# Turning two of four heads' softmax weights by VectorE blocks and DMA in the third attention of a four-layer conditioned sequence model

## The chip, the cores and the metric

The kernel runs on one core of one Trainium2 chip, as one program. The metric is the device time of one execution in microseconds (us). A program on one core is timed several times and the median is used; beside it there is one profiled execution, from which the page and every answer of the trace come.

A core has five engines with a queue of instructions each: TensorE (PE; its weight loads, PEld, overlap the matmuls), VectorE (DVE), ScalarE (ACT), GpSimd (POOL) and SyncE (SP), which here issues every DMA.

## The reference, cut to what matters

The input is `x` of 8 items with 256 tokens of 512 features. Four layers run in turn: a grouped attention with gated feed-forward (8 query heads, one key head), an attention with 16 heads and a feed-forward, the attention below, and a layer of small experts. The third layer is what the change bears on:

```python
h = h * (1.0 + scale[:, None, :]) + shift[:, None, :]      # h: layer norm of x
q = (h @ Wq.T).reshape(B, T, N_HEADS, HEAD_DIM).transpose(0, 2, 1, 3)      # 16 heads of 32
c_kv = h @ Wkd.T
k = (c_kv @ Wku.T).reshape(B, T, N_KV_HEADS, HEAD_DIM).transpose(0, 2, 1, 3)   # 4 heads
v = (c_kv @ Wvu.T).reshape(B, T, N_KV_HEADS, HEAD_DIM).transpose(0, 2, 1, 3)
...
scores = jnp.einsum('bhtd,bhsd->bhts', q, k_exp) / jnp.sqrt(jnp.asarray(HEAD_DIM, x.dtype))
scores = jnp.where(mask[None, None], jnp.asarray(-jnp.inf, x.dtype), scores)
attn = jax.nn.softmax(scores, axis=-1)
y = jnp.einsum('bhts,bhsd->bhtd', attn, v_exp)
out = y.transpose(0, 2, 1, 3).reshape(B, T, C) @ Wo.T
return x + out
```

The mask hides every key block of 128 that lies after the query's block. So the first 128 queries see 128 keys, the second 128 see 256.

## The kernel before, in words

**Layout.** Tokens are kept in 16 tiles of 128 tokens x 512 features in SBUF (`x`), two tiles (TB = 2) to an item. All arithmetic is fp32. The three attentions share one routine, `attend` (line 652 on). "Item" below means one of the 8 batch items, and "group" four heads of it that are worked on together. The third attention ("attention2", called in `layer2`, line 1673) has 4 groups an item, so 32 groups.

**One group.** `scored` (line 680; matmuls L692) gives the scores of four heads, queries on partitions, in four PSUM banks. `softmax` (line 698) has VectorE add the mask and find each row's maximum in one masked reduce per head and query block (L730), and ScalarE take the exponential with its row sum (L734). In this attention a head has 128 + 256 = 384 columns. The weights must then stand with the keys on partitions, as the second matmul sums over keys. There are two ways for that:

- *By TensorE* (`turned`, line 764). Each 128x128 tile is transposed by a matmul with the identity into a PSUM bank (L769), three tiles a head here, and the bank is copied back to SBUF by `copy` (line 474): VectorE for an even index (L478), ScalarE for an odd one (L481). The index starts at 0 with four such heads and at 1 with two.
- *By blocks* (in `softmax`, L739 to L743). Two heads' exponentials are written interleaved in 32-column blocks into one tile; VectorE transposes all its 32x32 blocks in one instruction (L739); four DMAs write it to a DRAM buffer, exchanging blocks (`put`, line 542, issued at L546); one DMA reads it back (L743). For this the heads' keys are read in another order in `scored`, and the bias or mask must be in the same order (`biased[1]`).

`weighted` (line 776, matmuls L794) multiplies values and turned weights: for each key tile the heads 0 to 3 in turn. `divided` (L811) divides by the row sums, which come by a small transposition (L745, L749) and two DMAs (L752, L757). `in_blocks` (line 538) says how many of the four heads go by blocks: two in the first and second attention, except in the last item, and none in the third.

**The order.** The loop of `attend` is pipelined by one group: scores of group i, first half of the turning of group i-1, softmax of group i, second half of the turning of i-1, weighting of i-1. Between these steps `some(quantum)` takes pieces of other work from a queue of Python generators: the output product of the item before (`added`, line 1288), the projections of the next item (`project2`, line 1633), and extra work. A generator yields the time it estimates for a piece, or None, after which `some` (line 207) ends; the forced `rest()` at each item's first group empties the queue and doesn't end on None.

**The tokens of an item ahead.** At an item's first group `prepare` (line 517) is begun for the item after next: `norms` (line 439) finds means and variances and normalises two token tiles into the buffer `hT`, yielding before each of them; then VectorE transposes hT's blocks (L532) and `put` writes it to DRAM. One step of it is taken per group. `fetch` (line 550), called once a group, reads it back with eight DMAs (L564), and `modulate` applies scale and shift at the item's last group (L488, L489).

**What is issued.** The text's order is not the issued order: a planner (the framework's scheduler) orders each engine's instructions by the text's order as priority and by when it expects them to be ready. `keep_in_program_order` (line 587, and line 803 for the weighting of heads that go by blocks) holds an instruction behind what stands before it on its engine in the text.

**The rotary tables** of the first layer are made by `angles` (line 1153) with VectorE and ScalarE: for the first item's tiles before the loop, and for the last 12 tiles in `conditions(0)` (line 1298), a generator queued behind the projection of item 1.

Of the kernel before, what the change touches and what calls it, by code (L numbers as in the profile page):

```python
# [34 lines left out]
P = 128  # L35
B, S, D = 8, 256, 512
NT = B * S // P
# [55 lines left out]
def in_blocks(m):  # L93

    return np.ascontiguousarray(m.reshape(-1, TB, 4, 32).transpose(0, 2, 1, 3).reshape(len(m), -1))


def constants():

    f32 = np.float32  # L100
    freqs = (f32(1.0) / f32(10000.0) ** (np.arange(0, 32, 2, dtype=f32) / f32(32))).astype(f32)
    ang = np.arange(S, dtype=f32)[:, None] * freqs[None, :]
    cos = np.cos(ang.astype(np.float64)).astype(f32)
    sin = np.sin(ang.astype(np.float64)).astype(f32)
    rope = np.stack([np.concatenate([cos, cos], 1), np.concatenate([-sin, sin], 1)], 1)
    rope = rope.reshape(TB, P, 2, 32).transpose(1, 0, 2, 3)
    i, k = np.arange(S)[:, None], np.arange(S)[None, :]
    hidden = ((np.abs(k - i) > 64) & (k % 64 != 0)) | (k // P > i // P)
    mask = np.where(hidden, f32(MASKED), f32(0.0))
    mask = np.concatenate([mask[:P, :P], mask[P:, :]], 1)  # L110
    return {
        "inv_freq": np.array([INV_FREQ], f32),
        "rope2": np.ascontiguousarray(rope),
        "mask2": np.ascontiguousarray(mask),
    }


# [61 lines left out]
class Program:  # L179
    def __init__(self, ctx, tc, d, out):  # L180
        self.ctx, self.tc, self.nc, self.d, self.out = ctx, tc, tc.nc, d, out
        self.n = 0
        self.queue, self.credit = [], 0.0
        self.ready, self.calls = {}, 0

    def pool(self, name, psum=False):
        return self.ctx.enter_context(
# [251 lines left out]
    def norms(self, xs, eps, rms=False, outs=None):  # L439


        nc = self.nc
        n = len(xs)
        mv = self.t([P, n, 2], f"mv{n}", 2)
        r = self.t([P, n], f"r{n}", 2)
        for i, x in enumerate(xs):
            st = self.t([P, 6], "st", 3)
            nc.vector.bn_stats(st, x)  # L448
            nc.vector.bn_aggr(mv[:, i, :], st)  # L449
        mean, var = mv[:, :, 0], mv[:, :, 1]  # L450
        if rms:
            nc.vector.tensor_tensor(r, mean, mean, ALU.mult)
            nc.vector.tensor_tensor(r, r, var, ALU.add)
            nc.gpsimd.tensor_scalar(r, r, eps, None, ALU.add)
        else:
            nc.gpsimd.tensor_scalar(r, var, eps, None, ALU.add)  # L456
        nc.gpsimd.tensor_tensor(r, r, self.neg_half[:, 0:n], ALU.pow)
        rows = []
        for i, x in enumerate(xs):
            yield  # L460
            if outs is None:
                y = self.bank("n")
            else:
                y, x = outs[i], x.rearrange("p (k c i) -> p c k i", k=KC, c=4)
            if rms:
                nc.vector.tensor_scalar(y, x, r[:, i : i + 1], None, ALU.mult)
            else:
                nc.vector.tensor_scalar(
                    y, x, mv[:, i, 0:1], r[:, i : i + 1], ALU.subtract, ALU.mult
                )  # L470
            rows.append(y)
        return rows
# [64 lines left out]

    def in_blocks(self, name, b):

        return 2 if name != "attention2" and b < B - 1 else 0  # L540

    def put(self, kept, tile):

# [6 lines left out]
    def fetch(self, calls):  # L550

        for (name, b), entry in self.ready.items():
            hT, _, kept, _, _ = entry
            if kept is None:
                continue
            entry[2:4] = None, self.calls + calls
            if self.stage(name)[5]:
                self.nc.sync.dma_start(hT, kept)
                continue
            parts = kept.rearrange("p (a k t j) -> p k t a j", a=4, k=KC, t=TB)  # L560
            to = hT.rearrange("p (k t a j) -> p k t a j", k=KC, t=TB, a=4)
            for k in range(KC):
                for t in range(TB):
                    self.nc.sync.dma_start(to[:, k, t], parts[:, k, t])  # L564

# [584 lines left out]

    def angles(self, cos, sin, tiles):

        nc = self.nc
        n = tiles.stop - tiles.start
        shape = [P, n, 32]
        cos, sin = cos[:, tiles], [s[:, tiles] for s in sin]
        pos = self.t([P, NT], "posf", 1)[:, 0:n]
        nc.vector.tensor_copy(pos, self.pos[:, tiles])  # L1160

        ang, high, rest = sin[1], sin[0], cos
        low = self.t([P, NT, 32], "n")[:, 0:n]
        nc.vector.tensor_tensor(
            ang,
            pos.unsqueeze(2).to_broadcast(shape),
            self.inv_freq.unsqueeze(1).to_broadcast(shape),
            ALU.mult,
        )

        def rounded(k, of, period):
            nc.vector.tensor_scalar(k, of, 1.0 / period, ROUND, ALU.mult, ALU.add)
            nc.vector.tensor_scalar(k, k, ROUND, None, ALU.subtract)

        def less(out, k, c):
            nc.vector.scalar_tensor_tensor(out, k, -c, ang, ALU.mult, ALU.add)

        rounded(high, ang, PERIOD)
        for c in HIGH[:3]:
            less(ang, high, c)  # L1180
        less(rest, high, sum(HIGH[3:]))
        rounded(low, rest, 2 * math.pi)
        for k, c in (
            (low, LOW[0]), (high, HIGH[3]), (low, LOW[1]), (high, HIGH[4]), (low, LOW[2]),
            (high, HIGH[5]),
        ):
            less(ang, k, c)

        rounded(low, ang, 2 * math.pi)
        less(ang, low, LOW[0])  # L1190
        less(ang, low, LOW[1] + LOW[2])
        nc.vector.tensor_scalar(ang, ang, PI_BELOW, -PI_BELOW, ALU.min, ALU.max)
        nc.scalar.activation(sin[0], ang, AF.Sin, scale=-1.0)
        nc.scalar.activation(rest, ang, AF.Abs)
        nc.scalar.activation(sin[1], ang, AF.Sin)
        nc.scalar.activation(cos, rest, AF.Sin, bias=self.half_pi, scale=-1.0)
# [98 lines left out]
    def layer0_attention(self):  # L1295
        self.ups = []

        def conditions(b):
            if b == 0:
                self.angles(self.cos, self.sin, slice(2 * TB, NT))  # L1300
                yield None
                yield from self.ada_1()
                yield from self.ada_0(1)
                self.ada_23_load()
            else:
                yield from self.ada_23()

                self.ups += [[None, None] for _ in range(8)]
                for i in (0, 1, 2, -1, 3, -2, -3, -4):
                    self.layer0_up(i if i >= 0 else -1 - i, int(i >= 0))  # L1310

        self.attend(
            "attention0", 2, 64, self.project0, lambda v, g, j, k: v[:, k, :],
            lambda b, ctxT: self.added(b, ctxT, self.w0o), (10.5, 6.8),
            extra={
                0: (conditions(0), 7.7), 2: (conditions(2), 4.6),
                5: (self.sums_of_ups(0, 2), 0.0), 6: (self.sums_of_ups(2, 4), 0.0),
                7: (self.mlp_input("mlp0"), 0.0),
            },
            then=lambda: self.mlp_begin("kept0"),  # L1320
            spare=lambda: [self.ups[i][1][:, 7, :] for i in range(4)],
            inverse=[self.w0[:, k, 640:896] for k in range(4)], after="mlp0",
        )
# [294 lines left out]
    def load_layer2(self):  # L1618
        nc, d = self.nc, self.d
        w = self.t([P, KC, 1536], "wqkv", pool=self.wqkvp)  # L1620
        self.load(w[:, :, 0:512], "wq2T")
        self.load(w[:, :, 512:640], "wkdT")
        nc.sync.dma_start(w[:, 0, 640:896], d["wkvuT"])
        self.w2 = w
        self.w2o = self.t([P, KC, D], "wo", pool=self.wop)
        self.load(self.w2o, "wo2T")
        rope = self.bank("row")[:, 0 : TB * 64].rearrange("p (t c s e) -> p t c s e", t=TB, c=2, s=2)
        nc.sync.dma_start(rope.rearrange("p t c s e -> p t c (s e)"), d["rope2"])
        self.rope2 = rope
        self.mask = self.bank("row")[:, :384]  # L1630
        nc.sync.dma_start(self.mask, d["mask2"])

    def project2(self, b, got):
        nc, w = self.nc, self.w2
# [38 lines left out]
    def layer2(self):  # L1673
# [2 lines left out]
        self.attend(  # L1676
            "attention2", 4, 32, self.project2, lambda v, g, j, k: v[:, k, j * 32 : (j + 1) * 32],
            lambda b, ctxT: self.added(b, ctxT, self.w2o), (10.4, 6.8), key_tiles=(1, 2),
            biased=(self.mask,), extra={7: (self.expert_inputs(0), 1.74)},
            spare=lambda: [spare[:, i, :] for i in range(4)],  # L1680
            inverse=[spare[:, i, :] for i in range(4, 8)],
        )
# [180 lines left out]
```

## Time and profile before

| what | value |
|---|---|
| median of 3 runs | 2106.18 us (2105.13 to 2107.4) |
| the profiled execution | 2102.78 us |
| its span, first to last instruction | 2100.7 us |
| mean granted TensorE clock | 0.989 of full speed |
| third attention, first scores to last weighting | 1673.5 to 1949 us |
| second attention, likewise | 913.3 to 1262 us |
| one item of the third, in the steady part | 34.4 us |
| one item of the second | 43.6 us |

How to read the page: its first part gives each engine's busy time and share of the span. The groups of instructions name line, engine, operation, output<-inputs by the program's tile names, shape and count, then busy time, the mean of one in ns, the idle time of the engine before them, and what ended it. In a timeline each row has a start and a length in us and may merge several instructions (x6); a note in brackets is the idle time before it and what released it. L794 and L692 appear twice per matmul of the program, so 16 records are 8 matmuls. Matmuls overlap in the array, so a record's length is not what one adds.

Some groups of the page on which this case turns:

```profile
L769 PE MATMUL C<-ident,p 128*128 128x128 f32 x816 | 122.3, 282 | 4.8 <-DVE p L478 1.9 <-ACT qT L482 1.5 <-ACT p L734 0.8
L734 ACT ACTIVATE p<-p,low 128x256 f32<-128x256 f32 (+1 forms) x512 | 240.0, 471 | 165.8 <-DVE low L730 154.5
```

L769 are the transposes by TensorE of all three attentions, 384 of the 816 in the third. In their row the idle time ahead of them is 4.8 us in all. The second row is the exponentials; ScalarE's idle time before them is mostly waiting for the reduces.

### The profile page before, as it was taken

The page shows a single profiled execution, that of the slowest core. Times are in us where ns is not written, and L with a number is a line of the kernel's source. Part 1 is how long each engine was busy: PE and PEld are TensorE (multiplying, and loading weights), DVE is VectorE, ACT ScalarE, POOL GpSimd, SP SyncE. Part 2 cuts the span into 40 slices and gives each one's busy share as a digit, 9 for nine tenths or more (in the row PEclk, how much of TensorE's full clock was granted, in tenths as well). Part 3 has the DMA queues.
Part 4 walks back from the last instruction along what each step waited for, and adds up shares of the span by engine and source line. Part 5 has one row for each costly group of instructions (what it writes and reads, how often), then busy time and mean ns, then how long its engine had stood idle before and what let it go on. Part 6 is the DMA issues. An engine that isn't in the chain of part 4 may idle for free.

```text
span 2100.7 us, 36220 instructions
## 1 busy us (share of the span) xinstructions
PE 2034.6 (97%) x12946; PEld 1486.9 (71%) x12946; DVE 1348.9 (64%) x4432; ACT 743.7 (35%) x2330; POOL 302.7 (14%) x340
## 2 busy tenths in 40 slices
PE   7799999999999999999999999999999999999999
PEld 4455569999999999854544448999999755555444
DVE  6677766666676555756676675767666777676233
ACT  4233421111111111146566652222222265556543
POOL 1111200000000000054445621000000111010220
PEclk8999999999999999999999999999999999999999
DMA  9543451212130010335455542235211321210001
GB/s 317 161 139 94 115 202 39 72 42 64 62 108 26 16 32 16 97 95 140 130 145 142 150 132 87 86 92 155 63 46 36 89 44 38 58 38 21 9 36 40
DMA packets 202659, 182.48 MB, mean 87 GB/s; under 512 B 81200, under 2 KB 169200, under 8 KB 202480
## 3 DMA queue, kind: packets, MB, share of 16 engines
q1 hardware_dynamic: 202480, 180.17, 29.3%
q8 instruction: 103, 1.69, 0.3%
q14 instruction: 76, 0.62, 0.1%
HBM read 122.16 MB, written 57.97 MB: 86 GB/s over the span
## 4 chain that ended last, share of the span: by engine, by line
PE 82%; DVE 6%; ACT 6%; DMA 3%; POOL 2%; issue 1%; SPq 0%; ACTq 0%; DVEq 0%; POOLq 0%
PE C L1002 28%; PE C L628 21%; PE A L1051 18%; ACT p L734 4%; PE A L692 4%; PE C L794 3%; PE C L769 3%; PE A L1731 1%; PE C L1750 1%; ACT p L481 1%; DVE st L448 1%; DVE p L730 1%; DMA hT<-turn 1%; PE C L315 1%; DVE n L647 1%
## 5 line engine op out<-in xcount | busy, mean ns | idle before, releaser
L1002 PE MATMUL C<-hT,wbig 128*128 128x128 f32 x3072 | 416.4, 275 | 1.0 <-DVE p L1025 1.0
L1002 PEld LDWEIGHTS C<-hT,wbig 128*128 128x128 f32 x3072 | 388.7, 192 | 10.1 <-issue 3.5
L628 PE MATMUL C<-wqkv,hT 128*128 128x512 f32 (+1 forms) x768 | 314.7, 551 | 0.4 <-ACT v L1490 0.4
L734 ACT ACTIVATE p<-p,low 128x256 f32<-128x256 f32 (+1 forms) x512 | 240.0, 471 | 165.8 <-DVE low L730 154.5
L1051 PE MATMUL A<-wbig,p 128*128 128x256 f32 x1024 | 242.2, 379 | 0.0
L628 PEld LDWEIGHTS C<-wqkv,hT 128*128 128x128 f32 x768 | 131.7, 193 | 122.7 <-issue 108.7
L1051 PEld LDWEIGHTS A<-wbig,p 128*128 128x128 f32 x1024 | 189.7, 190 | 23.1
L1032 DVE TENSOR_TENSOR p<-p,C 128x256 f32<-128x256 f32 x192 | 79.0, 419 | 164.3 <-PE C L1002 162.3
L1022 ACT COPY p<-C 128x128 f32<-128x128 f32 x192 | 50.8, 265 | 367.5 <-PE C L1002 359.0
L628 PE MATMUL C<-wo,ctxT 128*128 128x512 f32 x336 | 159.8, 609 | 2.9 <-DVE ctxT L811 2.9
L1002 PE MATMUL C<-ctxT,wbig 128*128 128x128 f32 x1152 | 160.0, 275 | 0.0
L1002 PE MATMUL C<-qk,wbig 128*128 128x128 f32 x1152 | 159.8, 275 | 0.0
L456 POOL TENSOR_SCALAR r<-mv 128x2 f32<-128x2 f32 (+1 forms) x28 | 7.0, 252 | 967.7 <-DVE mv L449 967.7
L730 DVE CUSTOM_DVE_ANT_0 p<-A,row 128x256 f32<-128x256 f32 (+1 forms) x400 | 127.8, 377 | 26.6 <-PE A L692 24.9
L1002 PEld LDWEIGHTS C<-ctxT,wbig 128*128 128x128 f32 x1152 | 144.1, 192 | 0.0
L1002 PEld LDWEIGHTS C<-qk,wbig 128*128 128x128 f32 x1152 | 144.0, 192 | 0.0
L769 PEld LDWEIGHTS C<-ident,p 128*128 128x128 f32 x816 | 92.2, 142 | 64.3 <-issue 37.8
L769 PE MATMUL C<-ident,p 128*128 128x128 f32 x816 | 122.3, 282 | 4.8 <-DVE p L478 1.9
L1374 ACT ACTIVATE p<-C 128x128 f32<-128x128 f32 x64 | 17.7, 277 | 302.4 <-DVE p L1032 302.4
L1023 DVE TENSOR_TENSOR p<-p,C 128x128 f32<-128x128 f32 x192 | 54.7, 285 | 96.6 <-ACT p L1022 95.6
L628 PEld LDWEIGHTS C<-wo,ctxT 128*128 128x128 f32 x336 | 59.5, 191 | 67.7 <-issue 55.2
L734 ACT ACTIVATION_READ_ACCUMULATOR p<-p,low 128x1 f32 x512 | 96.2, 188 | 0.0
(227 smaller groups left out, 3224.6 us busy)
## 6 DMA issues: line engine op xcount, KB each, us to landing
flip<-p SPq DMA_DIRECT2D x168, 128.0 KB
p<-flip SPq DMA_DIRECT2D x42, 512.0 KB
turn<-hT SPq DMA_DIRECT2D x120, 128.0 KB
hT<-turn SPq DMA_DIRECT2D x16, 512.0 KB
kept<-hT SPq DMA_DIRECT2D x16, 512.0 KB
hT<-kept SPq DMA_DIRECT2D x16, 512.0 KB
wbig<-spread SPq DMA_DIRECT2D x64, 128.0 KB
hT<-turn SPq DMA_DIRECT2D x112, 64.0 KB
```

The costliest lines, as they stand in the source:

```text
L315: self.nc.tensor.matmul(m[32 * i : 32 * i + 32, :], cond[:, k, :], w[c // 512][:, k, c % 512 : c % 512 + width], start=(k == 0), stop=(k = ...
L628: self.nc.tensor.matmul(out, lhsT(k), rhs(k), start=(k == 0), stop=(k == n - 1))
L692: nc.tensor.matmul(s[j][:, at[q] : at[q] + wide[q]], lhsT(q), keys, start=True, stop=True,)
L730: nc.vector.tensor_tensor_reduce(out, src, by, -1.0, BIG, ALU.add, ALU.min, low[:, q : q + 1])
L734: nc.scalar.activation(out, src, AF.Exp, bias=low[:, q : q + 1], scale=sign, accum_out=tot[:, j, q : q + 1],)
L769: nc.tensor.transpose(m[:, n * P : (n + 1) * P], p[:, at[q] + k * P : at[q] + (k + 1) * P], self.ident,)
L794: mm = nc.tensor.matmul(o[i * hd : (i + 1) * hd, c * S + q0 * P : (c + 1) * S], value(got[b][1], g, j, k), weights(j, mine), start=(k == 0 ...
L1002: nc.tensor.matmul(m[:, c : c + P], w[:, k * P : (k + 1) * P], b[:, k], start=(first and k == 0), stop=(k == steps - 1), skip_group_check= ...
L1022: nc.scalar.copy(g[:, 0, :], m[:, 0:P])
L1023: nc.vector.tensor_tensor(g[:, 0, :], g[:, 0, :], m[:, P : 2 * P], ALU.add)
L1032: nc.vector.tensor_tensor(g[:, 1:3, :], g[:, 0, :].unsqueeze(1).to_broadcast([P, 2, P]), m[:, 2 * P : 4 * P].rearrange("p (i t) -> p i t", ...
L1051: nc.tensor.matmul(acc[at][:, half * S : (half + 1) * S], left, right, start=(p == 0 and half == 0), stop=(p == 3), skip_group_check=True,)
```

## The change

1. `in_blocks` no longer excludes the third attention: in items 0 to 6 heads 0 and 1 of each group go by blocks. The mask is given in block order as well (`mask2_blocks`, a new constant of 128 x 384), and one bank now holds the rotary rows and the mask, the other the mask by blocks.
2. `norms` yields only before the second tile, so the first tile is normalised in the step that finds the statistics.
3. `fetch` reads an item's eight pieces in two calls of four, unless one of them is asked for at once or the whole is one DMA; the time from which it may be used is set at the second.
4. `angles` is a generator in four steps (`angle_steps`), and `conditions(0)` yields after each.

```diff
+        "mask2_blocks": np.concatenate([mask[:, :P], in_blocks(mask[:, P:])], 1),
...
         for i, x in enumerate(xs):
-            yield
+            if i > 0:
+                yield
...
     def in_blocks(self, name, b):
 
-        return 2 if name != "attention2" and b < B - 1 else 0
+        return 2 if b < B - 1 else 0
...
-            entry[2:4] = None, self.calls + calls
-            if self.stage(name)[5]:
+            whole = self.stage(name)[5]
+            ks = self.fetching.pop((name, b), range(KC if calls == 1 or whole else KC // 2))
+            if ks.stop == KC:
+                entry[2:4] = None, self.calls + calls
+            else:
+                self.fetching[name, b] = range(ks.stop, KC)
+            if whole:
                 self.nc.sync.dma_start(hT, kept)
                 continue
...
-            for k in range(KC):
+            for k in ks:
                 for t in range(TB):
                     self.nc.sync.dma_start(to[:, k, t], parts[:, k, t])
...
-    def angles(self, cos, sin, tiles):
+    def angles(self, *args):
+        for _ in self.angle_steps(*args):
+            pass
+
+    def angle_steps(self, cos, sin, tiles):
...
             if b == 0:
-                self.angles(self.cos, self.sin, slice(2 * TB, NT))
+
+                yield from self.angle_steps(self.cos, self.sin, slice(2 * TB, NT))
                 yield None
...
-        self.mask = self.bank("row")[:, :384]
+        self.mask = both[:, TB * 64 :]
         nc.sync.dma_start(self.mask, d["mask2"])
+        self.mask_blocks = self.bank("row")[:, :384]
+        nc.sync.dma_start(self.mask_blocks, d["mask2_blocks"])
...
-            biased=(self.mask,), extra={7: (self.expert_inputs(0), 1.74)},
+            biased=(self.mask, self.mask_blocks), extra={7: (self.expert_inputs(0), 1.74)},
```

`angle_steps` has three bare `yield`s: after the first reductions, and twice within and after the second ones.

## The prediction

> **What bounds the kernel now.** I read the page's engine row first, then the table by stretches for one batch item of the grouped attention (the third, of masked keys, 1673 to 1949 us), then the timelines of TensorE and ScalarE inside it, then the same views of the second attention, which already does what this change adds.
>
> ```profile
> span 2100.7 us, 36220 instructions
> PE 2034.6 (97%) x12946; PEld 1486.9 (71%) x12946; DVE 1348.9 (64%) x4432; ACT 743.7 (35%) x2330; POOL 302.7 (14%) x340
> ```
> TensorE is the bound over the whole span, so work taken from it looks like time. In the stretch that changes, one item (us, then busy us of PE, PEld, DVE, ACT, POOL, clock, DMA) has 1.5 us in 34.4 in which it isn't busy:
>
> ```profile
> 1779.50:1813.90 34.40, 32.85 (x232) 17.96 (x232) 24.76 (x114) 19.53 (x77) 4.30 (x6) 1.00 0.22 49
> ```
> Where these lie decides this case. TensorE's timeline of two weightings (L794) of that item:
>
> ```profile
> 1801.47 1.99 PE L628 MATMUL C<-wqkv,hT 128*128 128x512 f32 x4
> 1803.38 0.86 PE L794 MATMUL C<-p,v 128*32 128x256 f32 x16
> 1804.17 0.94 PE L692 MATMUL A<-v,qT 32*128 32x128 f32 x16
> 1805.04 0.87 PE L769 MATMUL C<-ident,p 128*128 128x128 f32 x6
> 1805.75 1.88 PE L628 MATMUL C<-wqkv,hT 128*128 128x512 f32 x4
> 1807.46 0.82 PE L769 MATMUL C<-ident,p 128*128 128x128 f32 x6
> 1808.12 0.60 PE L1652 MATMUL C<-wqkv,n 128*128 128x256 f32 x2
> 1808.75 0.63 PE L794 MATMUL C<-p,v 128*32 128x256 f32 x6
> 1809.92 0.84 PE L794 MATMUL C<-p,v 128*32 128x256 f32 x10 [0.54 <-ACT p L481]
> ```
> The first runs through in 0.86 us. The second stops after 6 of its 16 records, until ScalarE has copied the fourth head's turned weights. ScalarE's timeline shows why it is late:
>
> ```profile
> 1807.29 0.45 ACT L481 COPY p<-C 128x384 f32<-128x384 f32 x1
> ...
> 1809.32 0.19 ACT L734 ACTIVATION_READ_ACCUMULATOR p<-p,low 128x1 f32 x1
> 1809.41 0.46 ACT L481 COPY p<-C 128x384 f32<-128x384 f32 x1
> ```
> Eight exponentials and two copies run there without a gap, 4.76 us from the end of the scores (1805.1) to the end of the second copy. Measured so, from the end of the next group's scores, the four weightings of an item begin at +5.49, +5.42, +3.65 and +4.29 us, and the copy ends at +4.76, +4.56, +4.76 and +4.76: **slack 0.73 and 0.86, stall 1.1 and 0.5 us**. These repeat within 0.02 us in items 1 to 5. In item 6 two weightings stall and two have 0.05 us; in item 0 none has slack.
>
> **The change, part by part.**
>
> *Turning two of four heads elsewhere (items 0 to 6, 28 groups).* Removed: 6 of 12 transposes a group (L769). Their record says 0.28 us each, but they overlap: runs of 4 and of 8 take 0.66 and 1.09 us, so one costs 0.108 and six 0.65; 28 x 0.65 = 18.2 us of TensorE. Two VectorE copies of 0.55 go as well; ScalarE keeps both of its copies, since with two plain heads the index in `turned` gives both to it. So its 4.76 us stay, and six transposes fewer only count where a weighting has slack: the first two of an item, in items 1 to 5: 10 x 0.65 = **6.5 us**. In the other 18 groups TensorE arrives earlier and waits longer.
>
> On this the Trainium skill says ("TensorE: Matmul & The Clock Gate", Part 4: PE-mode transpose) that a 128x128 transpose takes about 275 ns inside a kernel. The records agree (273 ns median), the pitch in a run doesn't: by the page 28 x 6 x 0.275 = 46 us would leave TensorE, as an estimate.
>
> *Between two items* the scheduler fills a wait for the query copies with transposes: three, then two that wait 0.25 us for ScalarE's query copy, then the scores at 1813.89. With only three left to move there the scores can begin at 1813.53: 0.36 us, six times, **2.2 us**; 0 if other work is put in their place, 4.6 if ScalarE's first copy then also precedes its exponentials (about 0.4 more each).
>
> *What is added.* VectorE: one transpose of 128x768 a group. 128x1024 takes 1.245 us (L739), so 0.93, against 1.09 of copies: -0.16 us. VectorE is busy 24.8 of 34.4 us, so this is nothing in itself. The forms by blocks (runs of 32 or 64 elements) cost no more: in the second attention, where both occur, a weighting matmul takes 379 ns in either, a score matmul 374, an exponential 494 and 495, a masked reduce 419. SP: four writes (0.43 us each) and one read (0.34) a group, 2.1 us. TensorE's first weighting matmul now waits for that read. Behind it stand all of TensorE's later matmuls, and for them everybody.
>
> *When that read lands.* The trace has it in the second attention:
>
> ```profile
> 1175.08 1.25 DVE L739 STREAM_TRANSPOSE p<-p 128x1024 f32<-128x1024 f32 x1 [0.22 <-ACT p L734]
> ```
> ```profile
> 1176.35 1.75 SPq L546 DMA_DIRECT2D flip<-p  x4
> 1178.14 0.55 SPq L752 DMA_DIRECT2D spread<-invT  x1
> 1179.69 0.30 SPq L546 DMA_DIRECT2D turn<-hT  x1
> 1180.62 0.34 SPq L743 DMA_DIRECT2D p<-flip  x1
> ```
> Scores ended at 1172.0. Transpose at +3.1, writes from +4.3, landed at +8.5, read issued at +8.6, landed at +13.1. Over items 1 to 5 the medians of the landing are +13.4, +13.1, +12.6 and +13.1 for an item's four groups. In the grouped attention half of the reduces are 0.14 us shorter (-0.55), the transpose is 0.31 shorter, and the read is 384 KB instead of 512 (the 42 reads took 3.35 to 5.4 us, I take 0.4 off): 1.25 us earlier, so **+12.15, +11.85, +11.35, +11.85**. TensorE wants them, with the saving made, at 8.5 + 4.8 = +13.3, 8.55 + 4.8 = +13.3, 6.45 + 4.5 = +10.95, and 9.4 + 4.3 = +13.7 (distance to the next scores, plus the weighting's place; where ScalarE's copy binds, its end less 0.25). Only the third group is late, by 0.4 us: six times with item 6, 2.4 us. Item 6's first group (wanted at +11.0) adds 0.6. The very first group came at +17.1 in the second attention, here +15.9 against +14.8: 1.1. Sum **4.1 us lost**. Bounds: 1.1 if the reads land 0.4 us earlier, 12 if 1 us later.
>
> Against the whole idea the skill warns ("VectorE: DVE Perf Modes", The three transpose paths) that a plain strided DMA used as a transpose is 19 times slower than the crossbar's 1309 ns. As an estimate that is 25 us; every group would then wait over 10 us. The landing of 3.35 to 5.4 us speaks against it: these transfers move whole runs of blocks.
>
> *Tokens' blocks read by halves, norms one step earlier.* Eight reads (0.63 us on SP) become four and four; the first rows are written one group sooner. What is executed isn't the text's order: SP issues L752 before L743 above, though the text has it later. The rows are normalised when the hT buffer comes free (1779.4, just before the scores), reads issue from 1791 to 1798, and modulation uses them at 1812: 11 us of cover. Cost 0. Without cover a late read holds up VectorE and ScalarE, at most the 2.9 us for which SP once waited there. I take 0, between 1 us gained (SP freer for the new transfers) and 1 lost.
>
> *Rotary tables in steps.* The call that runs them is the forced `rest()` of item 1: the four calls of `some` in item 0 are spent on the four empty yields of the projection ahead in the queue, and `rest()` doesn't stop at empty yields. The tables' VectorE work stands at 58 to 65 us, ahead of item 1's first scores at 75, and its order stays as it is: 0.
>
> *Mask.* One more load of 192 KB. Today's mask is loaded at 1272 us and first used near 1679; the new one goes with it, and 400 us cover it: 0.
>
> **Sum.** -6.5 - 2.2 + 4.1 = -4.6 us. The profiled execution took 2102.78 us, its span 2100.7 and 2.1 around it; it becomes 2098.2. The median shown, 2106.18, is 3.4 us above that execution; the same difference gives **2101.6 us**.
>
> **Rivals.**
> *A, the whole saving:* the scheduler lets ScalarE's second copy pass the last exponentials, now that VectorE feeds them without two copies between, or reads land early. Then 18.2 us and the boundary's 2.2 go less the 1.1 at the start: down to 2087; from 2097 down counts here. For it: PE at 97%. Against: ScalarE's unbroken 4.76 us.
> *B, nothing:* ScalarE's chain and the late read eat all but 2 us either way, 2104 to 2108. For it: stall and gain are of one size.
> *C, slower:* VectorE puts the new transpose behind the reciprocal (L745), which stands at +4.45 waiting for the last exponential. The read then lands 1.9 us later than I reckon: third groups lose 2.3 us (six times, 13.8), first and second ones 0.75 and 0.45 (five times each, 6.0), item 6's first 2.5, the start 3: 25.3 - 8.7 = +16.6, or 2123. It decides from 0.6 us of delay on, where loss equals gain. For it: SP has eight further issues an item and the landings spread by 2 us. Against: in the second attention VectorE does this transpose before the reciprocal.
>
> **Chances.** Forecast (2098 to 2105) 0.50, of which 0.31 lies over 0.2% below the median and 0.19 within it; A 0.19; B 0.11; C 0.20. A measurement of this kernel can tell about 0.2%, 4.2 us. So faster 0.50, within 0.30, slower 0.20. The range, 2093 to 2113, leaves out about half of A and half of C.
>
> **What would show it.** Six-record runs of L769 become runs of three. The first two weightings of an item begin 0.65 us sooner; the other two still stop for ACT p L481. The waits table gets a row of L794 waiting for the DMA p<-flip, under 5 us in all. The new transposes stand near +2.9 of their scores, before L745. Were it over 10 us, or L739 behind L745, C is right; if the wait for L481 disappears, A.

## The result, and the profile after

| | before | after |
|---|---|---|
| median of 11 runs each | 2105.45 us | 2109.56 us |
| profiled execution, its span | 2102.78, 2100.7 us | 2109.53, 2107.4 us |
| third attention, first scores to the next layer's first matmul | 267.6 us | 272.7 us |

The ratio is 1.0020, 95% interval 1.0011 to 1.0029: **slower by 0.2%**, about 4 us, where 4.6 us less was forecast. Line numbers move with the edits; in the changed kernel L699 are the scores (L692 before), L776 TensorE's transposes (L769), L801 the weighting (L794), L548 all block writes, L571 the reads of the tokens' blocks, L750 the read of the turned weights (L743).

The page of the changed kernel, first lines:

```profile
span 2107.4 us, 36234 instructions
## 1 busy us (share of the span) xinstructions
PE 2020.4 (96%) x12778; PEld 1476.4 (70%) x12778; DVE 1352.2 (64%) x4404; ACT 744.6 (35%) x2330; POOL 303.8 (14%) x340
```

TensorE has 14.2 us less to do, and the span is longer: the time went into idle TensorE. Of the 6.7 us between the two profiled executions 5.1 lie in the third attention. Up to there TensorE's and VectorE's planned orders are those of before, and a kernel with the other parts of the change alone (below) is as fast as before. The item lengths, from one item's first scores to the next's:

| item | 0 | 1 | 2 | 3 | 4 | 5 | 6 | 7 |
|---|---|---|---|---|---|---|---|---|
| before | 37.4 | 34.1 | 34.4 | 34.4 | 34.4 | 34.4 | 28.9 | 29.4 |
| after | 41.0 | 29.7 | 35.8 | 33.4 | 37.8 | 32.7 | 27.0 | 35.3 |

Items 1, 3 and 5 gain 1.0 to 4.4 us, items 2 and 4 lose 1.4 and 3.4, item 0 loses 3.6, and items 6 and 7 together 4.0. The waits of TensorE in this attention, some of the longest (us in total, times, longest):

```profile
PE C L801 <- DMA p<-flip: 25.6, 10, 6.1
...
PE A L699 <- DVE qT L481: 3.6, 1, 3.6
PE C L801 <- ACT p L483: 1.3, 4, 0.7
```

The wait for the read of the turned weights is the new one, 25.6 us where under 5 was forecast. TensorE's timeline in item 2, which answers to the two weightings shown of before:

```profile
1768.25 0.86 PE L801 MATMUL C<-p,kT 128*32 128x256 f32 x16
1769.04 0.94 PE L699 MATMUL A<-kT,qT 32*128 32x128 f32 x16
1769.90 0.55 PE L776 MATMUL C<-ident,p 128*128 128x128 f32 x3
1770.29 1.88 PE L635 MATMUL C<-wqkv,hT 128*128 128x512 f32 x4
1772.01 0.49 PE L776 MATMUL C<-ident,p 128*128 128x128 f32 x3
1772.33 0.60 PE L1669 MATMUL C<-wqkv,n 128*128 128x256 f32 x2
1777.70 1.51 PE L801 MATMUL C<-p,kT 128*32 128x256 f32 x16 [4.77 <-DMA p<-flip]
```

Runs of six transposes have become runs of three. The second weighting, of the item's third group, stands 4.77 us for its read. SP's timeline of the same time says why it is late, and a second stretch, in item 6, shows another form of it:

```profile
1766.74 0.78 SPq L548 DMA_DIRECT2D flip<-p  x2
1767.63 2.56 SPq L571 DMA_DIRECT2D hT<-turn  x4
1770.23 1.09 SPq L548 DMA_DIRECT2D flip<-p  x2
1771.42 0.56 SPq L759 DMA_DIRECT2D spread<-invT  x1
1772.03 1.88 SPq L571 DMA_DIRECT2D hT<-turn  x3
1774.08 0.49 SPq L750 DMA_DIRECT2D p<-flip  x1
...
1904.35 1.76 SPq L548 DMA_DIRECT2D flip<-p  x4
1906.15 0.53 SPq L759 DMA_DIRECT2D spread<-invT  x1
1910.39 0.30 SPq L548 DMA_DIRECT2D flip<-p  x1
1910.93 0.34 SPq L750 DMA_DIRECT2D p<-flip  x1
```

The group's scores ended at 1763.5; times with a plus sign count in us from the end of a group's scores. VectorE's block transpose was done at +3.2. Seven reads of the tokens' blocks, 4.4 us of SP, stand among the four writes and ahead of the read, which is issued at +10.6 and lands at +14.1. In item 6 the group's own four writes have landed by 1907.7, but one write of the *next* group's weights, which waits for VectorE until 1910.39, stands ahead of this group's read at 1910.93. So a transfer that is ready waits on SP's list for one that isn't.

Theory 1, tested below: the saving is real, and SP's order gives it back; a long stop also halves the clock for a while. Theory 2: by ScalarE's chain there is no saving even with reads in time. Theory 3: the other parts of the change bring the loss.

### The profile page after: what moved, and what is told of

It is laid out like the page before. It is cut to its first block, busy times and chain, and to the rows that moved or that the text cites. A ratio compares the mean times of both kernels' runs of the same rounds, so it can differ in the third digit from the quotient of the medians.

```text
span 2107.4 us, 36234 instructions
## 1 busy us (share of the span) xinstructions
PE 2020.4 (96%) x12778; PEld 1476.4 (70%) x12778; DVE 1352.2 (64%) x4404; ACT 744.6 (35%) x2330; POOL 303.8 (14%) x340
## 3 DMA queue, kind: packets, MB, share of 16 engines
q1 hardware_dynamic: 222784, 202.40, 32.7%
## 4 chain that ended last, share of the span: by engine, by line
PE 79%; DVE 6%; ACT 6%; DMA 4%; issue 1%; POOL 1%; SPq 1%; ACTq 0%; DVEq 0%; POOLq 0%
PE C L1009 28%; PE C L635 19%; PE A L1058 18%; ACT p L741 4%; PE A L699 4%; PE C L801 4%; PE C L776 2%; DMA p<-flip 1%; PE A L1748 1%; DVE p L737 1%; ACT p L483 1%; PE C L1767 1%; DVE st L449 1%; DMA hT<-turn 1%; PE C L316 1%
## 5 line engine op out<-in xcount | busy, mean ns | idle before, releaser
L776 PEld LDWEIGHTS C<-ident,p 128*128 128x128 f32 x648 | 75.0, 143 | 59.1 <-issue 38.1
L776 PE MATMUL C<-ident,p 128*128 128x128 f32 x648 | 103.3, 285 | 3.2 <-ACT p L741 1.9
L699 PE MATMUL A<-kT,qT 32*128 32x256 f32 (+2 forms) x896 | 90.0, 402 | 8.2 <-DVE low L737 4.9
```

Source lines behind the costliest of these rows:

```text
L699: nc.tensor.matmul(s[j][:, at[q] : at[q] + wide[q]], lhsT(q), keys, start=True, stop=True,)
L776: nc.tensor.transpose(m[:, n * P : (n + 1) * P], p[:, at[q] + k * P : at[q] + (k + 1) * P], self.ident,)
```

## The experiments

Each time is a median; a ratio stands to the kernel before, with its 95% interval.

**One part at a time.** `e1_blocks_only` takes back the edits of `norms`, `fetch` and `conditions`, `e2_rest_only` that of `in_blocks`; the last pair of lines is of the second kernel:

```diff
-            if i > 0:
-                yield
+            yield
...
-            ks = self.fetching.pop((name, b), range(KC if calls == 1 or whole else KC // 2))
+            ks = range(KC)
...
-        return 2 if b < B - 1 else 0
+        return 2 if name != "attention2" and b < B - 1 else 0
```

> The weights of two heads by VectorE blocks and DMA, with the second mask, and nothing else of the change: the norms, the one read of the tokens' blocks by eight transfers and the rotary tables are as in the kernel before. Theory 1 (the way by blocks saves TensorE time, but SP issues transfers of the tokens' blocks among the new writes and reads, so that some reads land 3 to 4 us late, and each stop of TensorE of 4 us or more is followed by a stretch at half clock): the eight reads stand in front of the same reads, so the loss stays, 2107 to 2113 us, with 30 to 50 us of waits of the weighting for the read back of the blocks. Theory 2 (ScalarE's chain eats the saving even where the reads are in time): 2104 to 2107. Theory 3 (the halves and the earlier norm bring the loss): 2098 to 2103, below the kernel before.

> The other parts of the change without the blocks in the third attention: norms one step earlier, tokens' blocks read by halves, rotary tables in steps, the second mask loaded. Theories 1 and 2: within 1.5 us of the kernel before, 2104 to 2107. Theory 3 (these parts bring the loss): 2108 to 2111.

Blocks alone: 2111.8 us, 1.0030 (1.0019 to 1.0042). The rest alone: 2105.2 us, 0.9996 (0.9987 to 1.0005). Theory 3 falls: the blocks bring the loss. But in the first of them the wait for reads is only 15.1 us, half of what I expected there. Its late reads are mostly those of the fourth groups (+15.5 to +19.3 in items 2 to 5), and VectorE begins block transposes at up to +5.3 in items 3 to 5 and +8.0 in item 6, which the changed kernel begins by +2.6. So late reads are not all of the loss in this kernel; how it divides was not followed.

**Without the tokens' round trip.** In `prepare`, for the third attention from item 2 on:

```diff
+        if name == "attention2" and b >= 2:
+            self.ready[name, b][3] = self.calls + 3
+            return
         self.put(kept, hT)
```

> The changed kernel without the round trip of the tokens' blocks through memory in the third attention (items 2 to 7): the four writes and eight reads an item are left out, so the tokens stay in unexchanged blocks and the output isn't the reference's. SP then has only the blocks of weights, the spread and the broadcasts. Theory 1: no read of the weights lands past +12.5 us of its scores after item 0, waits of the weightings for it under 8 us, no half-clock stretch in items 1 to 6 of this attention, 2094 to 2100 us. Theory 2: the stalls go, the time stays at 2103 us or more, since ScalarE's copies still end at +4.76. Theory 3 has no number of its own for it, 2100 to 2106.

2096.8 us, 0.9958 (0.9944 to 0.9972). In items 1 to 5 reads land at +9.6 to +11.3, and items 2 to 5 take 31.6 to 31.9 us. Theory 2 falls: with reads in time an item saves 2.7 us. Not as expected: items 0 and 7 still cost 3.2 and 5.4 us more than before (items 6 and 7 together 3.3), a half-clock stretch follows a stop in each, and the wait for reads is 10.7 us, not under 8.

**Another form of the same reads** (one transfer per block row instead of one per column and tile):

```diff
-            for k in ks:
-                for t in range(TB):
-                    self.nc.sync.dma_start(to[:, k, t], parts[:, k, t])
+            for a in range(4):
+                self.nc.sync.dma_start(dst[:, a, m], src[:, a, m])
```

> The changed kernel with each half of the tokens' blocks read in four transfers of half the... same bytes each, one for every block row instead of one for every column of blocks and tile; since a half now has two columns and two tiles, it is four transfers as well, but the source is read in runs of 512 B and no longer 128 B. SP issues as many as before. Theory 1: SP's issue time is what stands ahead of the reads, so nothing much changes, 2107 to 2111 us, unless a transfer's issue is cheaper by its form, then 2104 to 2107. Theory 2: 2109.

2107.4 us, 1.0008 (0.9998 to 1.0017): as many transfers, about 2 us less than the changed kernel. Items 2 and 4 still take 35.7 and 35.5 us, so the form of the reads is not what makes them late.

**The round trip on another engine.** `put` and `fetch` issue the tokens' transfers of the third attention by ScalarE, or by GpSimd:

```diff
-                    self.nc.sync.dma_start(to[:, k, t], parts[:, k, t])
+                    on = self.nc.gpsimd if name == "attention2" else self.nc.sync
+                    on.dma_start(to[:, k, t], parts[:, k, t])
```

> The changed kernel with the round trip of the tokens' blocks in the third attention issued by ScalarE and no longer by SP (twelve transfers an item, from item 2 on); the weights' writes and reads stay on SP. Theory 1 (SP's order makes the reads late): SP is as free as without the round trip, the reads land by +12.5 us, items 1 to 5 take about 31.7 us each as there, 2096 to 2101 us. Its weak point: the reads of the tokens' blocks wait for their own writes, and on ScalarE such a wait holds up exponentials; if that decides, 2105 to 2115, with exponentials that start late and weightings that wait for ScalarE. Theory that the load of the transfers on the DMA engines, not the order on SP, makes the reads late: they stay late, 2107 to 2112.

> The same round trip issued by GpSimd, which does six things an item here. Theory 1: reads by +12.5 us, 2096 to 2101 us, unless GpSimd's issue of a transfer takes so long that the rotations' sums (which the queries of the next item wait for) come late; then 2103 to 2110. Theory of the load on the DMA engines: 2107 to 2112.

By GpSimd 2096.6 us, 0.9959 (0.9945 to 0.9974). By ScalarE 2109.5 us, over a wide span (2101.5 to 2112.5). Its profile is of the shortest run, so what makes the others 8 us longer is not shown. In that profile ScalarE waits 8.8 us with exponentials behind reads of tokens and 5.7 us with a copy behind writes of tokens that wait for VectorE's transpose: in kind the weak point named. SP with the round trip on GpSimd, the same group of item 2 (scores ended at 1761.6):

```profile
1764.90 1.77 SPq L548 DMA_DIRECT2D flip<-p  x4
1766.71 0.53 SPq L760 DMA_DIRECT2D spread<-invT  x1
1768.33 0.35 SPq L751 DMA_DIRECT2D p<-flip  x1
```

The read is issued at +6.7 and lands at +9.8. The same bytes move, so the load on the DMA engines was not the cause. A stretch of one item each (us, then busy us of PE, PEld, DVE, ACT, POOL, clock, DMA share, GB/s), items 2 and 3 of the changed kernel:

```profile
1745.60:1781.50 35.90, 30.67 (x208) 16.29 (x207) 28.13 (x116) 19.41 (x78) 5.41 (x8) 0.92 0.53 138
1781.50:1814.90 33.40, 30.44 (x213) 15.97 (x212) 23.64 (x106) 19.78 (x79) 3.55 (x4) 0.98 0.54 141
```

and with GpSimd's round trip:

```profile
1743.70:1775.40 31.70, 29.98 (x207) 15.49 (x206) 25.14 (x111) 19.42 (x78) 12.53 (x18) 1.00 0.55 150
1775.40:1807.20 31.80, 30.09 (x211) 15.56 (x210) 24.66 (x110) 19.51 (x78) 12.54 (x18) 1.00 0.58 154
```

TensorE's idle time in an item is 1.7 us, against 1.55 before and 5.2 in item 2 of the changed kernel, while its work fell by 2.8: nearly all of the saving arrives. GpSimd is busy 12.5 us an item for it where it was 4.3 before, and TensorE's list of waits there has no row for GpSimd, where before it began with one:

```profile
PE C L1236 <- POOL qk L1650: 4.4, 6, 0.8
```

**The order on SP.** All stays on SP, but a group's writes and spread are put behind the read of the group before, and the tokens' writes and reads behind the last read traced; the tokens' reads are traced after the softmax. The order of issue alone is asked for:

```diff
+    def behind(self, name, issue, read=None):
+        read = read or self.last_read
+        if name == "attention2" and read is not None:
+            with self.tc.issue_after(read.ins):
+                issue()
...
-                    self.put(kept, blocks)
-                    nc.sync.dma_start(blocks, kept)
+                    self.behind(name, lambda: self.put(kept, blocks))
+                    self.last_read = nc.sync.dma_start(blocks, kept)
```

> The changed kernel with every transfer still on SP and in the same number, but in another order in the third attention: the writes of a group's weights and its spread are issued behind the read of the group before, and the reads of the tokens' blocks behind the read of the group with which they are traced (they are traced after that group's softmax). Theory 1 (order on SP): the reads issue at about +7 us of the scores in items 1 to 5 and land by +11.5, these items take about 31.7 us each, the time is that of the round trip on GpSimd, 2095 to 2099 us. Theory that two engines' issuing side by side is what helped there: SP still issues as much, the reads stay 1 to 4 us late, 2104 to 2110.

> The same order on SP, with the blocks in items 1 to 5 alone. In the run with the round trip on GpSimd item 0 took 3.1 us more than before, items 6 and 7 together 3.5, items 1 to 5 saved 13.8. If the three parts stand by themselves, items 0, 6 and 7 go back to their times before: 2091 to 2094 us. If the loss of item 0 is the price of a first item and moves to item 1: 2094 to 2098. If order isn't enough: 2104 or more, as with the blocks in items 1 to 5 and the order as planned (2113.5).

2116.3 us, 1.0050 (1.0036 to 1.0064), and 2111.2 us, 1.0026 (1.0015 to 1.0037): the first lies outside both theories, the second where order isn't enough. Yet in items 1 to 5 of the first the reads land at +9.6 to +12.6, no longer at +14 or +15. VectorE's timeline between items 4 and 5, and TensorE's below it, show the new loss:

```profile
1857.14 1.50 DVE L471 TENSOR_SCALAR hT<-x,mv,r 128x512 f32<-128x512 f32 x2
1858.67 1.24 DVE L535 STREAM_TRANSPOSE hT<-hT 128x1024 f32<-128x1024 f32 x1
1859.84 0.38 DVE L830 TENSOR_TENSOR ctxT<-C,wbig 128x256 f32<-128x256 f32 x1
1860.15 0.67 DVE L482 TENSOR_SCALAR qT<-C 128x512 f32<-128x512 f32 x1
```
```profile
1860.37 0.30 PE L1270 MATMUL C<-ident,kr 128*128 128x128 f32 x1 [1.90 <-DVE ctxT L830]
```

With the reads moved in the text the planner put the norm and transpose of a later item's tokens, 2.7 us, ahead of a division that TensorE's next PSUM bank and the next scores waited for (5.8 us in all, against 0.4 in the changed kernel). So SP's order was mended and VectorE's broken. With the norms held behind the block transpose of the item's first group on VectorE as well:

```diff
+                    self.tc.add_manual_dep(
+                        made.ins, flip.ins.name,
...
+                        reason="behind the blocks",
+                    )
```

> All transfers on SP in the mended order, and VectorE's norms of the tokens of item b+2 behind the block transpose of the first group of item b. Theory 1 (order is the cause): reads by +12.6 us and no wait for a division between items; items 1 to 5 at 31.7 to 32.5 us, 2095 to 2100 us. Theory that SP has not enough room for the transfers: 2104 or more, with reads late again.

> The same with the blocks in items 1 to 5 alone. Theory 1: as with the round trip on GpSimd in the same items, 2090 to 2094 us. Theory that SP has not enough room: 2100 or more.

2100.6 us, 0.9975 (0.9965 to 0.9985), and 2098.3 us, 0.9973 (0.9963 to 0.9983). With as many transfers on the same queue as in the changed kernel, order is worth 9 us and makes it faster than before. The edit orders both SP and VectorE; since the changed kernel loses only 0.4 us to such divisions, the 9 us are put down to SP's order, though VectorE's was not tried alone. Reads land by +11.8 in items 1 to 5; items 2 to 5 take 33 us, 1.3 more than with GpSimd, and the time is 0.6 us above the range of theory 1. What these 1.3 us are was not followed; in the second kernel they, and item 6 at 31.3 us, keep it above the 2090 to 2094 expected.

**Which items.** The blocks in some items of the third attention alone, first with the transfers as changed, then with the round trip on GpSimd (there for items 1 to 6, then 1 to 5):

```diff
+        if name == "attention2":
+            return 2 if 1 <= b <= 5 else 0
         return 2 if b < B - 1 else 0
```

> The changed kernel with the blocks in the third attention in items 1 to 5 alone; items 0 and 6 are turned by TensorE as before, everything else as changed. Without the round trip of the tokens' blocks item 0 still cost 3 us more than before and item 7, behind item 6, 5 us; these go. Theory 1: the late reads of items 2 and 4 stay, with a half-clock stretch after each, the odd items gain 1.5 to 4 us each: 2101 to 2106 us. Theory 2 (no gain by blocks): 2106 to 2109.

> The round trip of the tokens' blocks on GpSimd, blocks in items 1 to 6 (without item 0). By the parts of the run on GpSimd: 3 us less than that one's 2096.6, 2093 to 2095 us; if the loss of item 0 moves to item 1, 2096 to 2098.

> The round trip of the tokens' blocks on GpSimd, blocks in items 1 to 5. By the parts: 2105.5 - 13.8 = 2091.7, so 2090 to 2093 us, 2 to 3 us less than with item 6 as well; if only item 0's loss goes, or only moves, 2094 to 2098. The theory that the way by blocks has nothing to win (2): 2104 or more.

With SP's planned order 2113.5 us, 1.0033 (1.0021 to 1.0045), more than either theory gave: the wait for reads is 20.6 us again, and now the odd items are the late ones (35.3, 36.4 and 36.8 us). Which items suffer depends on the plan. With GpSimd 2095.8 us, 0.9957 (0.9941 to 0.9974) for items 1 to 6 and **2091.0 us, 0.9931 (0.9917 to 0.9946)** for 1 to 5, the best of all: 14 us below the kernel before, 22.5 below the same items with SP's planned order. Its item lengths are 38.1, 31.4, 31.7, 31.7, 31.7, 31.8, 29.1, 29.4: the losses of items 0, 6 and 7 go with their blocks, but for 0.7 us in item 0, and do not move to the neighbours. Items 1 to 6 came out 1 to 3 us worse than its parts promised.

**The clock.** Matmuls whose result is overwritten fill the long stops, so that TensorE isn't idle as long:

```diff
+            if (name, g) == ("attention2", 2) and b in (0, 2, 4):
+                self.fill(o, 6 if b < 4 else 7)
```

> The changed kernel with matmuls whose result is overwritten (identity by a column of weights, 128 by 512, six or seven in a row, about 2.8 or 3.3 us) put in front of the four stops of TensorE that are 3.6 us or longer: the weightings of the third group in items 0, 2 and 4, and the first scores of item 7. They do nothing but shorten the idle time. If the half-clock stretches come from the idle time (theory 1's second half): the four stretches of 6.83 us that the profile of the changed kernel has there go, each worth up to 3.4 us, and the time falls by 6 to 13 us, to 2097 to 2104, although work was added and the reads land as late as before. If the stretches don't follow from the idle time or cost nothing: 2109 to 2113.

> The round trip on GpSimd in all items with blocks (2096.6 us), and six matmuls without use (about 2.8 us) in front of the weighting of item 0's third group (where TensorE stood idle 5.7 us) and of item 7's first scores (3.6 us). SP's order is unchanged. Both half-clock stretches should go. If a stretch costs what it holds back, up to 3.4 us each: 2090 to 2094. If it costs about nothing, because TensorE isn't what is waited for just then: 2096 to 2098.

2118.3 us, 1.0063 (1.0048 to 1.0077), and 2099.1 us, 0.9971 (0.9962 to 0.9981). The totals mislead: in both, the fill ahead of item 7's first scores put these scores behind a weighting whose read is late (idle 5.8 and 6.9 us), and items 6 and 7 together grew by 6 us; in the first, reads of items 3 and 5 came late too (36.8 and 34.9 us). Item 0 can be read, with GpSimd's round trip without and with the fill, one fence each:

```profile
1672.10:1712.60 40.50, 29.67 (x181) 19.34 (x180) 34.74 (x128) 21.09 (x78) 13.66 (x21) 0.79 0.46 123
```
```profile
1673.60:1712.90 39.30, 33.09 (x194) 19.88 (x193) 34.45 (x128) 21.48 (x79) 12.98 (x19) 0.87 0.47 118
```

The clock rises from 0.79 to 0.87 since one stretch is gone, and the item gets 1.2 us shorter (1.0 in the other pair, 41.0 to 40.0). In item 2 the clock went from 0.92 to 1.00 and the time from 35.8 to 36.1, with a read 1.4 us later. So a stretch costs about 1 us where this could be measured, not the 3.4 of theory 1's second half. That TensorE is not what is waited for just after a stop would explain it, but was not tested. The loss of item 2 has the size by which its third group's weighting is late: it starts at +14.2 instead of +10.0, and the item takes 35.8 us instead of 31.8.

## Why the prediction was wrong

- **Six transposes, 0.65 us a group: right.** Runs of 0.87 and 0.82 us became 0.55 and 0.49.
- **"Only count where a weighting has slack": too small.** 1.66 us an item were forecast with the step between items, 2.7 came when the reads were in time. The first two groups gain 0.8 and 0.6 us and the third nothing, as reckoned. The fourth gains 0.4 us. The step between items gains 0.8, nearly all of it the wait for GpSimd's sum, which is gone and which I had not counted; the 4.4 us shown above are six such waits. The 0.36 us forecast for that step hardly shows: the scores begin earlier, but stop 0.37 us for ScalarE's query copy. The wait for ScalarE's copy of the turned weights stayed (0.64 us in item 2's third group), so rival A's mechanism is not what happened, though its size is close.
- **"When that read lands": the step that failed.** +12.15, +11.85, +11.35 and +11.85 were forecast from the second attention, with only the third group late, by 0.4 us. Without the tokens' round trip the reads land at +9.6 to +11.3 in items 1 to 5, up to 2.3 us before the forecast; with nothing between them, the four writes and the read need about 6.6 us from the end of the block transpose. In the changed kernel they land at +9.8 to +15.4 there, with the third groups of items 2 and 4 at +14.1 and +15.4. The step took for granted that SP's order would be that of the second attention. There the tokens' blocks are moved too, but the groups are 10.9 us apart, never more than three reads of tokens stand between a group's first write and its read, and all landings of items 1 to 5 lie between +11.9 and +13.6. In the third attention of the changed kernel the groups are 8 to 9 us apart on the average. Seven reads of tokens stand there in the third groups of items 2 and 4, and at most three in every other group. That order is what the borrowed stage doesn't show. 4.1 us of loss were forecast; against the run on GpSimd the changed kernel loses 12.3 in this attention, 10 of them in items 2 and 4.
- **"Tokens' blocks by halves: cost 0": right.** The rest alone is as fast as before, and beside the blocks the eight reads at once (2111.8 us) are no better than the halves (2109.6). I asked what a late read of tokens would cost and found 11 us of cover. I did not ask what those reads, in either form, do to the transfers behind them: that belongs to the step above.
- **First and last items: mis-sized.** 1.1 us were forecast for the very first group and 1.0 for item 6. With the round trip on GpSimd item 0 costs 3.1 us and items 6 and 7 together 3.6. In item 0 VectorE is busy 34.7 us against 29.4 before, and ordering SP did not mend it (41.1 us, although its third group's read then came at +10.1). In the changed kernel VectorE begins that group's block transpose at +5.3, against about +2.3 in items 1 to 5; behind item 6 the next scores wait 3.6 us for VectorE's query copy. Taking the blocks out of these items removes the loss but for 0.7 us. Its cause in item 0 was not tested further and stays open.
- **Rotary tables and mask at 0: right**, by the run of the rest alone. **VectorE and the forms by blocks at 0: right as far as the rows show.** The new transpose takes 0.98 us where 0.93 was reckoned, and a group's scores and weightings by blocks still take 0.94 and 0.86 us. In item 0 VectorE did matter, as said above.
- **Rival C: the right sign from another place.** The new transpose stands ahead of the reciprocal (1786.16 and 1787.92 in one group), so its mechanism did not happen; what made reads late was SP's list.
- **The Trainium skill's rule on a strided DMA as a transpose** ("VectorE: DVE Perf Modes", The three transpose paths), 19 times slower, had been set aside: rightly, a read lands about 3 us after its issue where nothing is in its way (3.1 in item 2's third group with GpSimd), and the late ones were late by their issue.

## What to carry to other kernels

A round trip through memory costs what its queue puts between its writes and its read: list every transfer on that queue with its planned place in the new stage, item by item, before an end-to-end time is borrowed from another stage. When a gain goes missing behind a DMA, leave out the *other* traffic of its queue first: one run tells the price. An independent round trip does well on the queue of an engine that nobody waits for, as GpSimd was here and ScalarE was not. And an edit that mends one engine's order can break another's: read all engines' timelines again after it.

## What the runs showed that was not expected

- Each of the five idle times of TensorE of 3.6 us or more in the changed kernel's third attention is followed by a stretch of 6.83 us at half clock, beginning 2.9 to 4.9 us after the idle time began; its idle times of 1.6 to 2.2 us there have none. The Trainium skill ("TensorE: Matmul & The Clock Gate", Why this matters for your kernels) says that no idle gap should exceed about 3 us, or the clock halves; that agrees. The price here, about 1 us a stretch, is less than the 3.4 us of work that a stretch at half clock holds back.
- The Trainium skill ("Trainium Kernel Development and Optimization", Key Constraints) says of the queues of SP, ScalarE and GpSimd that "issuing from several engines concurrently only saves the sequencer's issue time". In item 2 it was such issue time, seven reads of 4.4 us, that stood ahead of the late read; in item 6 it was the wait for a transfer that was not ready, which that sentence leaves out. Here the measurement decides. The small issue times had a large price: moving twelve transfers an item to GpSimd was worth 13 us, and another order with all of them on SP 9 us.
- GpSimd took 2.2 us to issue the tokens' four writes and 0.75 each for the reads, where SP took about 1.9 (0.47 each) and 0.63.
